# Band attention: weights of a 64-key half kept as 80 queries, sums and values as 64-row products in two slots around the next scores

## The chip, the cores and the metric

The kernel runs on one core of one Trainium2 chip. The metric is device microseconds for one execution, taken as the median of three runs. The kernel before takes 2633.2 us (the three runs: 2632.67, 2633.2 and 2638.77).

Engine names are those of the profile: PE is TensorE (matrix products), PEld its weight loads, DVE is VectorE, ACT is ScalarE, POOL is GpSimd, and SP issues the DMAs. Results of matrix products land in PSUM, which has eight banks of 128 partitions by 512 float32.

## The reference

The input is (2, 256, 128, 128) float32: batch, time, frequency, channel. Three blocks follow each other, each with a layer norm in front and a residual add behind it: attention over time (causal), attention over frequency (a band of 16 to each side), and a feed-forward net with gelu. Both attentions have four heads of 32 channels.

```python
xt = _ln(x, ln_t_w, ln_t_b).transpose(0, 2, 1, 3)
x = x + _mha(xt, t_wi, t_bi, t_wo, t_bo, H_T, cm).transpose(0, 2, 1, 3)   # causal
xf = _ln(x, ln_f_w, ln_f_b)
x = x + _mha(xf, f_wi, f_bi, f_wo, f_bo, H_F, bm)      # abs(i - j) <= 16
xn = _ln(x, ln_n_w, ln_n_b)
h = jax.nn.gelu(xn @ w1.T + b1, approximate=False)
x = x + (h @ w2.T + b2)
```

The change touches the second block alone, the band attention. There a sequence is 128 frequencies long, and a query sees only keys that are at most 16 away.

## The kernel before

Work goes in groups of 512 tokens (four sequences of 128). First come 128 groups of the time attention (class `OverTime`), then 16 runs, each of eight groups of the band attention (`OverBands`) and then eight of the feed-forward net (`FeedForward`). The loop in `run` walks over the groups; one turn n of it issues parts of several neighbouring groups, and `InOrder` pins every instruction to the place in its engine's queue where the program wrote it. So the order of calls in `run` is the order on each engine.

A float32 product on PE is written as one `matmul` and is recorded as two passes (two loads and two matmuls in the profile). The kernel always splits the array into smaller tiles which work side by side, one product in each. Three shapes matter here, written as rows (contracted) by columns (outputs):
- 128x32, four tiles, one for each head or each 32 output channels: projections, sums, values, output
- 32x64, eight tiles, four heads by two halves of the keys: scores
- 64x32, eight tiles, two halves of the keys by four heads: only in the change

What one band group does, in steps that the text below calls by these names:
- **projections** (`queries_keys`, `values`): qT and kT from two sets of four products of 512 columns, then v from 16 products of 128 columns. ACT takes them from PSUM.
- **scores** (`scores`): 32 products of 80 columns. A half of 64 keys meets only the 80 queries of its sequence that can be in its band; the bank holds 128 query columns for each sequence, and what lies outside the 80 is not written and masked later.
- **weights**: DVE puts the band of minus 1e30 on the last head (`scalar_tensor_tensor`, 128x512), ACT takes the exponential of all four heads (128x512 each), POOL then clears what is outside the band in the other three heads (`affine_select`, two each). The result is `pf`.
- **sums and values** (`weigh`): four products of 512 columns of `pf` with ones, then 16 of 128 columns of `pf` with v, over all 128 keys of a sequence.
- **division**: ACT takes ln and exp of the sums (`invert`, gives r), DVE refines and multiplies in three instructions (`divide`, gives oT).
- **output** (`output`, `finish`): 16 products of 128 columns, and the residual add on DVE.

In a turn n in the midst of a run the order on PE is: scores of group n, sums and values of n-1, output of n-2, queries and keys of n+1, values' projection of n+1. Where the first feed-forward group follows the last band group (`turn` in `run`), the sums and values of n-1 stand behind the hidden products of the feed-forward group.

PSUM banks are handed out in rotation (`turn_of_bank`), with some numbers reserved ahead (`held`, `follow`). A bank's next user waits until the last reader of the bank is done.

## Time and profile before

| | |
|---|---|
| median of three runs | 2633.2 us |
| span of the profiled execution | 2631.9 us |
| band groups, feed-forward groups, time groups | 128 each |
| sums of `pf`, passes of 128x512 | 1024, mean 603 ns |
| values of `pf`, passes of 128x128 | 4096, mean 273 ns |
| scores of the band groups, passes of 32x80 | 8192, mean 240 ns |
| `affine_select` on `pf`, POOL | 768, mean 637 ns |
| exponential to `pf`, ACT | 512, mean 602 ns |

The page of the profiled execution gives its span, from the first to the last instruction; the run's time has about 1.3 us beside it. A "mean" of a pass on PE is the time from its start to its end in the pipeline; since tiles work side by side and passes follow each other before they end, what a step costs is read from the starts of one step and the next in the timeline, and not from means times counts.

### The profile page before, as it was taken

The numbers are of one execution on the slowest core, as the hardware profiler recorded it, in microseconds if no ns is written. First come the engines' busy times: TensorE is split into PE (matmuls) and PEld (weight loads), VectorE is DVE, ScalarE is ACT, GpSimd is POOL, SyncE is SP. The second block draws the span as 40 slices with busy tenths as digits, with TensorE's granted clock in tenths as the row PEclk, the third lists the DMA queues.
The fourth block names the chain that finished last, engine by engine and source line by source line (L and its number), as shares of the span: only waits on it lengthen the run. The fifth ranks groups of instructions, "written<-read, shape, count | busy, mean of one in ns | idle before, by whom it ended". The sixth has DMA issues, their size and how long they took to land.

```text
span 2631.9 us, 156460 instructions
## 1 busy us (share of the span) xinstructions
PE 2617.8 (99%) x68688; PEld 1837.4 (70%) x68688; DVE 2140.8 (81%) x6410; ACT 1838.8 (70%) x3543; POOL 1958.6 (74%) x2311
## 2 busy tenths in 40 slices
PE   9999999999999999999999999999999999999999
PEld 6666666666766767666777776667676677777776
DVE  8888888888888887977878779788797797887974
ACT  7989988999899875564655746647557466475573
POOL 7999999999999987666667666665776666757762
PEclk9999999999999999999999999999999999999999
DMA  6656555565565454445454544554454445554543
GB/s 155 167 149 158 149 149 149 155 155 149 149 158 149 122 127 119 115 123 127 118 124 124 123 122 117 126 128 120 122 126 120 120 119 131 123 120 123 123 104 88
DMA packets 469797, 344.97 MB, mean 131 GB/s; under 512 B 43120, under 2 KB 404464, under 8 KB 469104
## 3 DMA queue, kind: packets, MB, share of 16 engines
q1 hardware_dynamic: 468408, 334.41, 50.5%
q8 instruction: 540, 8.85, 1.5%
q14 instruction: 153, 1.25, 0.2%
q10 hardware_dynamic: 696, 0.46, 0.1%
HBM read 167.98 MB, written 166.72 MB: 127 GB/s over the span
## 4 chain that ended last, share of the span: by engine, by line
PE 99%; DVE 0%; issue 0%; DMA 0%; ACT 0%; ACTq 0%; DVEq 0%
PE bank L907 99%; DMA x<-in_x 0%; DVE xh L907 0%; DVE bank L907 0%; DVE res L907 0%; DVE stats L907 0%; DVE oT L907 0%; DVE u L907 0%; DVE xnT L907 0%; ACTq L907 0%; ACT p L907 0%; DVE vy L907 0%; ACT lnv L907 0%; DVE mv L907 0%; ACT root L907 0%
## 5 line engine op out<-in xcount | busy, mean ns | idle before, releaser
L907 ACT ACTIVATE hT<-bank,b 128x512 f32<-128x512 f32 x512 | 348.1, 688 | 524.2 <-PE bank L907 483.2
L907 POOL TENSOR_SCALAR_AFFINE_SELECT pf<-pf 128x512 f32<-128x512 f32 x768 | 477.7, 637 | 185.3 <-ACT pf L907 159.1
L907 PEld LDWEIGHTS bank<-w2T_sb,hT 128*32 128x32 f32 x16384 | 467.4, 110 | 54.8 <-issue 29.0
L907 PE MATMUL bank<-xnT,wf 128*32 128x512 f32 x4096 | 492.4, 592 | 0.5 <-DVE xnT L907 0.5
L907 PE MATMUL bank<-xnT,w1f 128*32 128x512 f32 x4096 | 486.3, 592 | 0.2 <-issue 0.2
L907 PE MATMUL bank<-w2T_sb,hT 128*32 128x128 f32 x16384 | 482.8, 273 | 1.0 <-issue 1.0
L907 ACT ACTIVATE p<-bank 128x512 f32<-128x512 f32 (+1 forms) x1024 | 430.6, 494 | 62.9 <-PE bank L907 62.9
L907 DVE TENSOR_SCALAR xh<-x,mv,rstd 128x160 f32<-128x160 f32 (+1 forms) x1012 | 394.3, 432 | 59.7 <-POOL rstd L907 49.4
L907 POOL TENSOR_SCALAR_AFFINE_SELECT p<-p 128x1024 f32<-128x1024 f32 (+2 forms) x384 | 364.5, 949 | 57.5 <-ACT p L907 49.1
L907 PEld LDWEIGHTS bank<-wf,xnT 128*32 128x32 f32 x8192 | 243.3, 110 | 144.1 <-issue 101.6
L907 POOL TENSOR_TENSOR p<-p,p 128x512 f32<-128x512 f32 x256 | 324.6, 1291 | 10.6
L907 DVE BATCH_NORM_STATS2 stats<-x 128x6 f32<-128x128 f32 x1536 | 329.0, 276 | 3.4 <-DMA x<-in_x 3.4
L907 POOL TENSOR_SCALAR rstd<-mv 128x4 f32<-128x4 f32 x251 | 57.8, 230 | 361.7 <-DVE mv L907 360.5
L907 PEld LDWEIGHTS bank<-xnT,w1f 128*32 128x32 f32 x4096 | 183.6, 110 | 171.6 <-issue 109.6
L907 PE MATMUL bank<-qT,kT 32*64 32x80 f32 (+4 forms) x16384 | 302.0, 271 | 0.1
L907 PEld LDWEIGHTS bank<-qT,kT 32*64 32x64 f32 x16384 | 260.0, 131 | 51.2 <-ACT kT L907 50.6
L907 DVE TENSOR_TENSOR res<-bank,res 128x512 f32<-128x512 f32 (+1 forms) x259 | 170.3, 658 | 153.3 <-PE bank L907 144.7
L907 ACT ACTIVATE pf<-bank 128x512 f32<-128x512 f32 x512 | 265.8, 602 | 35.5 <-PE bank L907 31.3
L907 PE MATMUL bank<-wn,oT 128*32 128x128 f32 x8192 | 283.8, 274 | 0.1
L907 DVE STREAM_TRANSPOSE z<-xh 128x512 f32<-128x512 f32 x380 | 270.3, 711 | 13.3
L907 PE MATMUL bank<-wf,xnT 128*32 128x128 f32 x8192 | 276.5, 273 | 0.0
L907 POOL TENSOR_TENSOR rstd<-rstd,mhalf 128x4 f32<-128x4 f32 x251 | 260.8, 1039 | 20.9
(100 smaller groups left out, 3820.3 us busy)
## 6 DMA issues: line engine op xcount, KB each, us to landing
turned<-z SPq DMA_DIRECT2D x1520, 64.0 KB, 2.7
xnT<-turned SPq DMA_DIRECT2D x380, 256.0 KB, 3.2
x<-res SPq DMA_DIRECT2D x256, 128.0 KB, 2.5
x<-x SPq DMA_DIRECT2D x128, 256.0 KB, 4.1
out<-res SPq DMA_DIRECT2D x252, 128.0 KB, 2.3
x<-in_x SPq DMA_DIRECT2D x124, 256.0 KB, 4.3
x<-in_x SPq DMA_DIRECT2D x4, 128.0 KB, 2.8
x<-in_x SPq DMA_DIRECT2D x6, 64.0 KB, 2.9
```

Source lines behind the costliest of these rows:

```text
L907: return self.tc.keep_in_program_order(emit(*args, **kwargs))
```

## The change

The weights of a half of 64 keys are kept as 80 query columns (`REACH`), and so the scores' bank, the exponential and the masks handle 4 x 80 = 320 columns for each head. POOL multiplies with a constant `keep` of ones and zeros, once for a head in place of two selections. The head that DVE masks is now masked and exponentiated later in the turn (`late_mask`, `late_function`).

Sums and values are taken over 64 keys at a time, on 64x32 tiles, 80 queries each, and the two halves are added in PSUM where they overlap. The first slot (`weigh_first`) has the sums of the upper half and the values of the lower, the second slot (`weigh`) the sums of the lower and the values of the upper. The first slot of group n-1 stands ahead of the scores of n, the second behind them. At the end of a run the output of n-2 stands between the two slots. A copy of one column on ACT (`seen`) is issued behind the first slot, and the first product of the second slot waits for it.

Banks are no longer handed out in rotation but from a list of free ones, oldest first; each user gives its bank back when its last reader has been issued.

```diff
+REACH = HALF + BAND
-    by_vector = 1
+    by_vector = 3
-        self.sp = {h: path.bank([P, NT * P], "sp") for h in heads}
+        self.sp = {h: self.take(f"sp{h}", [P, NT, REACH]) for h in range(H)}
...
-                        self.sp[h][keys, q], self.kT[r, i * P + e * HALF : i * P + (e + 1) * HALF], self.qT[r, q],
-                        start=True, stop=True,
+                        self.sp[h][keys, i], self.kT[r, i * P + e * HALF : i * P + (e + 1) * HALF],
+                        self.qT[r, a : a + REACH], start=True, stop=True,
...
+    def first_mask(self):
+        path = self.path
+        keep = path.keep.unsqueeze(1).to_broadcast([P, NT, REACH])
+        for h in range(H):
+            if h != self.by_vector:
+                path.gpsimd.tensor_tensor(self.p[:, h], self.p[:, h], keep, ALU.mult)
...
+    def part(self):
+        path = self.path
+        seen = path.small.tile([P, 1], F32, name="seen")
+        self.seen = path.scalar.copy(seen, self.op_[:, NT - 1, 0:1])
...
+    def sums(self, e):
+        rows, a = slice(e * HALF, (e + 1) * HALF), e * (P - REACH)
+        for h in range(H):
+            m = self.path.tensor.matmul(
+                self.rp_[rows_of(h), :, a : a + REACH], self.path.k.ones[rows, 0:D], self.p[rows, h],
+                start=e == 1, stop=True, skip_group_check=True,
             )
+            if e == 0 and h == 0:
+                self.behind(m)
+
+    def weighted(self, e):
+        rows, a = slice(e * HALF, (e + 1) * HALF), e * (P - REACH)
         for i in range(NT):
             for h in range(H):
                 r = rows_of(h)
+                self.path.tensor.matmul(
+                    self.op_[r, i, a : a + REACH], self.v[rows, i, r], self.p[rows, h, i],
+                    start=e == 0 and i == 0, stop=True, skip_group_check=True,
+                )
+
+    def weigh_first(self):
+        self.rp_ = self.take("rp", [P, NT, P])
+        self.op_ = self.take("op", [P, NT, P])
+        self.rp, self.op = (t.rearrange("p i q -> p (i q)") for t in (self.rp_, self.op_))
+        self.sums(1)
+        self.weighted(0)
+        self.part()
+
+    def weigh(self):
+        self.sums(0)
+        self.weighted(1)
...
+            if bands[1] and bands[2]:
+                do(n - 1, "weigh_first")
             do(n, "first_half", "first_function", "first_mask")
...
+            do_at(n, OverBands, "late_mask")
+            if turn:
+                do(n - 1, "weigh_first")
+                do(n - 2, "output", "finish")
             do(n - 1, "weigh")
             do(n - 1, "invert_exactly" if turn else "invert")
+            do_at(n, OverBands, "late_function")
...
-            if bands[2] or turn:
+            if bands[2]:
                 do(n - 2, "output", "finish")
```

How this moves instructions is seen in three places, all in turns of the loop in the midst of a run. First PE, from the last two score products of a turn to the first ones of the next, before (`pf,ones` are the sums, `pf,v` the values, `wn` the output, `xnT,wf` queries and keys, `wf,xnT` the projection of v):

```order
L907 MATMUL bank_111<-qT,kT 64x80
L907 MATMUL bank_112<-qT,kT 64x80
L907 MATMUL bank_115<-pf,ones 32x512 x4
L907 MATMUL bank_108<-pf,v 32x128 x16
L907 MATMUL bank_113<-wn_241,oT 32x128 x16
L907 MATMUL bank_114<-xnT,wf_238 32x512 x4
L907 MATMUL bank_109<-xnT,wf_238 32x512 x4
L907 MATMUL bank_110<-wf_238,xnT 32x128 x16
L907 MATMUL bank_111<-qT,kT 64x80
L907 MATMUL bank_112<-qT,kT 64x80
```

and in the change:

```order
L968 MATMUL bank_114<-qT,kT 64x80
L968 MATMUL bank_115<-qT,kT 64x80
L968 MATMUL bank_109<-pf,ones 32x4x80 x4
L968 MATMUL bank_110<-pf,v 32x80 x16
L968 MATMUL bank_112<-wn_253,oT 32x128 x16
L968 MATMUL bank_113<-xnT,wf_250 32x512 x4
L968 MATMUL bank_111<-xnT,wf_250 32x512 x4
L968 MATMUL bank_108<-wf_250,xnT 32x128 x16
L968 MATMUL bank_114<-pf,ones 32x4x80 x4
L968 MATMUL bank_115<-pf,v 32x80 x16
L968 MATMUL bank_112<-qT,kT 64x80
L968 MATMUL bank_109<-qT,kT 64x80
```

The second slot of one group stands where sums and values stood, with 80 columns for 128; the first slot of the next group has come in ahead of the next scores. The scores now take banks 109 and 110, in which the sums and values of the group before were added up (their division reads them); before, they took other banks.

Second DVE, from one finished oT to the next, before (`band` is the mask, `xh` the normalization of a later group, `z` its transpose, `x` the residual add):

```order
L907 TENSOR_TENSOR oT<-bank_112,u 128x4x4x32
L907 SCALAR_TENSOR_TENSOR bank_110<-bank_110,band 128x512
L907 TENSOR_SCALAR xh<-x,mvs,rstds 128x5x32 x4
L907 STREAM_TRANSPOSE z<-xh 128x512
L907 TENSOR_TENSOR x_18417<-bank_111,x_18417 128x512
L907 TENSOR_TENSOR bank_113<-bank_113,r_20994 128x512
L907 SCALAR_TENSOR_TENSOR u<-bank_113,r_20994 128x512
L907 TENSOR_TENSOR oT<-bank_114,u 128x4x4x32
```

and in the change:

```order
L968 TENSOR_TENSOR oT<-bank_110,u 128x4x4x32
L968 TENSOR_SCALAR xh<-x,mvs,rstds 128x5x32 x4
L968 STREAM_TRANSPOSE z<-xh 128x512
L968 SCALAR_TENSOR_TENSOR bank_113<-bank_113,band 128x320
L968 TENSOR_TENSOR x_18429<-bank_111,x_18429 128x512
L968 TENSOR_TENSOR bank_114<-bank_114,r_21059 128x512
L968 SCALAR_TENSOR_TENSOR u<-bank_114,r_21059 128x512
L968 TENSOR_TENSOR oT<-bank_115,u 128x4x4x32
```

The mask has moved behind the normalization and its transpose, and has 320 columns.

Third ACT over one turn, before (`pf` are the exponentials):

```order
L907 COPY v<-bank_114 128x512
L907 ACTIVATE pf<-bank_115 128x512
L907 ACTIVATE pf<-bank_108 128x512
L907 ACTIVATE pf<-bank_109 128x512
L907 ACTIVATE pf<-bank_110 128x512
L907 ACTIVATE ln<-bank_113 128x512
L907 ACTIVATE r_20994<-ln 128x512
L907 ACTIVATE qT<-bank_112,bq_283 128x512
L907 COPY kT<-bank_115 128x512
```

and in the change:

```order
L968 COPY v<-bank_108 128x512
L968 COPY seen<-bank_115 128x1
L968 ACTIVATE pf<-bank_112 128x320
L968 ACTIVATE pf<-bank_109 128x320
L968 ACTIVATE pf<-bank_110 128x320
L968 ACTIVATE ln<-bank_114 128x512
L968 ACTIVATE r_21059<-ln 128x512
L968 ACTIVATE pf<-bank_113 128x320
L968 ACTIVATE qT<-bank_108,bq_295 128x512
L968 COPY kT<-bank_112 128x512
```

The copy `seen` stands ahead of the exponentials, and the last head's exponential has gone behind ln and r.

## The prediction, made before the change was run

> **What bounds the kernel now.** I read the page first: its busy shares and its chain.

> ```profile
> span 2631.9 us, 156460 instructions
> PE 2617.8 (99%) x68688; PEld 1837.4 (70%) x68688; DVE 2140.8 (81%) x6410; ACT 1838.8 (70%) x3543; POOL 1958.6 (74%) x2311
> PE 99%; DVE 0%; issue 0%; DMA 0%; ACT 0%; ACTq 0%; DVEq 0%
> ```

> PE is never idle and is the whole chain, so the change is worth what it does to PE, as long as no other engine takes over. Next the timeline of PE over one turn of the band stage, since the starts there give what each step costs:

> ```profile
> 1497.43 0.97 PE L907 MATMUL bank<-qT,kT 32*64 32x80 f32 x64
> 1498.33 1.06 PE L907 MATMUL bank<-pf,ones 128*32 128x512 f32 x8
> 1499.21 1.06 PE L907 MATMUL bank<-pf,v 128*32 128x128 f32 x32
> 1500.08 1.06 PE L907 MATMUL bank<-wn,oT 128*32 128x128 f32 x32
> 1500.95 1.90 PE L907 MATMUL bank<-xnT,wf 128*32 128x512 f32 x16
> 1502.67 1.06 PE L907 MATMUL bank<-wf,xnT 128*32 128x128 f32 x32
> 1503.66 0.97 PE L907 MATMUL bank<-qT,kT 32*64 32x80 f32 x64
> ```

> From start to start (us): scores 0.90, sums 0.88, values 0.87, output 0.87, queries and keys 1.72, projection of v 0.99; a turn is 6.23. Three things are to be seen. *The price of a column*: on each of four tiles the output makes 8 passes of 128 columns in 0.87 (109 ns a pass), queries and keys 4 of 512 in 1.72 (430 ns), so a pass costs a tile 0.84 ns a column and 2 ns: 69 ns for 80 columns, 0.27 us for 320. *A change of tile shape*: the projection of v has the same 32 passes as the output but costs 0.99, because another shape follows: 0.12 us. *A stall*: on eight tiles the 64 passes of the scores need 8 x 69 ns = 0.55 and cost 0.90.

> **The stall**, which decides this case. Narrow windows of the same timeline, up to 1503.99 and at 1503.99 and 1504.30 (rows begin with the first pass still under way):

> ```profile
> 1503.66 0.56 PE L907 MATMUL bank<-qT,kT 32*64 32x80 f32 x33
> 1503.78 0.85 PE L907 MATMUL bank<-qT,kT 32*64 32x80 f32 x56
> 1504.04 0.58 PE L907 MATMUL bank<-qT,kT 32*64 32x80 f32 x30
> L907 PE MATMUL bank<-qT,kT 32*64 32x80 f32 x8192 | 124.0, 240 | 0.1
> ```

> 33 passes, that is 17 products with their two, start in the first third of a microsecond. The next starts at 1504.04, 0.38 after the first. The first product's second pass starts at 1503.78 and takes about 0.23 (mean 240 ns), so it ends near 1504.01, 0.03 ahead. I read this as a queue with room for 17 products, filled while PE changes shape, in which a place is handed on 0.03 us after a product has ended; then the other 15 products enter at about 20 ns each.

> Are places handed on in program order, or as products end? In the band scores all products are alike and both give 0.90. In the time stage's scores they have 64 to 256 columns, and there it differs. I worked through their 32 products in the written order (`TIME_ORDER`), with the prices above: from the first score to the next step 1.30 us in program order, 1.18 in any order; the whole time turn 7.06 and 6.94.

> ```profile
> 501.67 1.39 PE L907 MATMUL bank<-qT,kT 32*64 32x64 f32 x64
> 502.98 1.08 PE L907 MATMUL bank<-wn,oT 128*32 128x128 f32 x32
> 508.75 1.14 PE L907 MATMUL bank<-qT,kT 32*64 32x64 f32 x41
> ```

> The rows have 1.31 and 7.08: program order. [...]

> **The change, PE.** A slot has four sums of 320 columns on one half of the rows and 16 values of 80 columns on the other. On eight tiles side by side a slot would need 2 x 0.27 or 8 x 69 ns: 0.55 us, where sums and values now have 1.75 together. But the sums stand first in program order and end late. Bounds of a 320-column pass from start to end:

> ```profile
> L907 PE MATMUL bank<-xnT,wf 128*32 128x512 f32 x4096 | 492.4, 592 | 0.5 <-DVE xnT L907 0.5
> L907 PE MATMUL bank<-p,ones 128*32 128x256 f32 x2048 | 134.0, 379 | 0.0
> L907 PE MATMUL bank<-pf,ones 128*32 128x512 f32 x1024 | 143.6, 603 | 0.0
> ```

> Between 379 ns at 256 columns and 592 at 512: 0.43 us at 320. The first sum's second pass starts at 0.29 (0.27 and some 0.025 for weights that could not be loaded ahead; 64-row tiles are not in this trace, and I take the 128-row ones, which have 32 columns too). It ends at 0.73, and its place goes on at 0.76. The queue holds four sums and 13 values. So the last three values enter at 0.76, 0.78 and 0.80, load for 0.03 and make two passes: the last pass starts at 0.90. By the rows of the scores the next shape starts 0.16 after the last pass. **A slot costs about 1.05 us**, 0.5 of it with most tiles empty.

> In a turn: scores 0.90 as before, 2 x 1.05 for 0.88 and 0.87, the rest unchanged (the 0.12 behind the projection of v stays; the change of shape behind each slot is in its 0.16). That is +0.35; worked through product by product it is 6.60 for 6.23, +0.37. There are seven such turns in each of 16 runs: 112 x 0.37 = **+41 us**. At a run's end the slots stand around the output, between steps of another shape: +0.35 and two changes at 0.12, 16 x 0.59 = **+9 us**. The bounds of a slot are 0.71 (0.55 + 0.16, no stall) and 1.27 (sums and values one after the other); I take 1.05, because the rule behind it gives 0.90, 1.31, 6.23 and 7.08 as the rows have them.

> **The other engines.** DVE now makes some turns longer than PE does:

> ```profile
> 1478.43 0.96 PE L907 MATMUL bank<-qT,kT 32*64 32x80 f32 x64
> 1484.97 0.97 PE L907 MATMUL bank<-qT,kT 32*64 32x80 f32 x64
> 1492.69 0.67 DVE L907 SCALAR_TENSOR_TENSOR bank<-bank,band 128x512 f32<-128x512 f32 x1
> 1497.57 0.69 DVE L907 TENSOR_TENSOR oT<-bank,u 128x512 f32<-128x512 f32 x1
> 1499.23 0.67 DVE L907 SCALAR_TENSOR_TENSOR bank<-bank,band 128x512 f32<-128x512 f32 x1
> ```

> Masks at 1492.69 and 1499.23 are 6.54 apart with DVE busy throughout, and one turn of PE is 6.54 (1478.43 to 1484.97). Such turns add some 0.6 us a run over 6.23, about 9 us in 16 runs (read alike in all runs; this row is one of them). With a mask of 320 columns for 512 DVE needs about 6.3. At 6.60 from PE it is no longer late: **-9 us**, at most; at least 0.

> New on the path could be the banks: scores of n+1 take the banks of the sums and values of n-1, and so wait for oT of n-1. That ends, after the scores of n start: scores 0.90, second slot with output 1.92, some 0.2, residual add 0.6 and three instructions at 0.7 each: 5.8. Against 6.60 that is free; it would decide in a shorter turn.

> ```profile
> L907 POOL TENSOR_SCALAR_AFFINE_SELECT pf<-pf 128x512 f32<-128x512 f32 x768 | 477.7, 637 | 185.3 <-ACT pf L907 159.1
> L907 POOL TENSOR_TENSOR p<-p,p 128x512 f32<-128x512 f32 x256 | 324.6, 1291 | 10.6
> L907 ACT ACTIVATE pf<-bank 128x512 f32<-128x512 f32 x512 | 265.8, 602 | 35.5 <-PE bank L907 31.3
> L907 ACT ACTIVATE p<-bank 128x256 f32<-128x256 f32 x512 | 183.6, 390 | 62.3 <-PE bank L907 62.3
> ```

> POOL's masks go from 6 x 0.64 = 3.8 to 3 x 0.81 = 2.4 (1291 ns by 320/512; between 0 and 3 x 1.29), ACT's four exponentials from 2.4 to 1.8 (0.44 each, between 390 and 602 ns). Both lie beside PE, and the first slot needs them only 5.6 after the scores start, so neither counts. The copy `seen` is bounded by 0 and a pass of 256 (390 ns); behind it on ACT stand the exponentials, which need the scores anyway, 0.9 later. Its waiter, the second slot, stands behind the scores: nothing. The late exponential stands behind ln and r and is done some 4 us after the scores start: nothing.

> Sum: 2631.9 + 41 + 9 - 9 = 2673 for the profiled span; with the 1.3 us by which the median lies above it, **2674**.

> **Rivals.**
> 1. *Places come free in any order, or 64-row tiles have more room.* Then a slot is 0.71, a PE turn 5.94, and DVE (6.3 with statistics) and the chain to oT (5.8 and a wait) set it to about 6.1, against 6.31 on average now (6.23 and 9 us over 112 turns). -0.2 x 112: 2610. For it: the eight tiles of the scores do run side by side. Against it: the 1.31 and 7.08. [...] Chance 0.15.
> 2. *The same, with the gain eaten* by DVE or by the wait for the banks: turns near 6.3, 2633 within 8. Chance 0.05.
> 3. *The wait for the banks decides too.* The row of the scores at 1491.20, to set beside that of oT at 1497.57 above:

> ```profile
> 1491.20 0.97 PE L907 MATMUL bank<-qT,kT 32*64 32x80 f32 x64
> ```

> There oT of n-1 ends at 1498.26, 7.1 after the scores of n start, with DVE late. In the change a normalization of 1.6 us and a transpose stand ahead of the mask; if DVE is late by them, this wait decides once oT ends more than 6.6 after its turn's scores start. Turns at 6.85 would give 112 x 0.25 more, 2702. Against it: DVE needs only 6.3. Chance 0.10.
> 4. *The row halves do not run side by side*, so that the change doesn't do what it says: a slot of 1.27, 128 x 2 x 0.22 more: 2730. For it: no row here has a 64-row tile. Against it: eight tiles of 32 rows do. Chance 0.04.

> **How the numbers follow.** The forecast, 2660 to 2690, has 0.66: places for 16 or 18 products move it by 4, the 9 us of DVE by 9. Rivals 1 and 2 have 0.20, rivals 3 and 4 0.14. The range from 2620 to 2705 takes in the forecast and rivals 2 and 3 (0.81), and leaves out rivals 1 and 4. Faster by over 0.3% (8 us, about what a measurement of this kernel can tell from no change): 0.15; within: 0.05; slower: 0.80.

> **What would show it.** In the changed kernel's timeline a slot should take 1.05 from its start to the next step, with 16 or 17 products started early, a gap until about 0.76, and then the last values; the next scores should keep 0.90, the turn should have 6.60. If slots have 0.7, the queue is not what I think; if slots have 1.05 and turns are longer than 6.7, look for loads of the scores that wait for DVE. I would be wrong most of all if 64-row tiles are handled otherwise than the two shapes that this trace has.

## The result, and the profile after

The changed kernel takes **2756.1 us** (median of four runs, 2749.0 to 2768.5) against 2633.4: a ratio of 1.047, with a 95% interval from 1.0446 to 1.0492. The forecast of a slower kernel was right, its size was not: 123 us where 41 were forecast, and outside the range. The profiled execution has a span of 2747.2 us, 115.3 above the one before.

The page of the changed kernel, its span, busy times, chain and the row of the DMA queue that brings instructions; the last row is that of the kernel before, for which the prediction did not quote it:

```profile
span 2747.2 us, 166900 instructions
PE 2688.8 (98%) x73808; PEld 1823.1 (66%) x73808; DVE 2124.2 (77%) x6410; ACT 1777.4 (65%) x3671; POOL 1804.0 (66%) x1934
q8 instruction: 581, 9.52, 1.6%
PE 95%; issue 2%; DVE 2%; DMA 0%; ACT 0%; SPq 0%; POOL 0%; ACTq 0%; DVEq 0%; POOLq 0%
```

```profile
q8 instruction: 540, 8.85, 1.5%
```

PE still is the chain, but it is no longer never idle: "issue", time in which it waits for nothing that the profile shows, has 2%. Two numbers will matter: PE has 5120 matmuls more, and as many loads, together 10240 records; and q8 has 41 packets more.

The timeline of PE over one undisturbed turn, to set beside the turn that the prediction shows:

```profile
1741.48 0.97 PE L968 MATMUL bank<-qT,kT 32*64 32x80 f32 x64
1742.38 0.47 PE L968 MATMUL bank<-pf,ones 64*32 64x320 f32 x4
1742.41 0.48 PE L968 MATMUL bank<-pf,v 64*32 64x80 f32 x16
1742.67 0.45 PE L968 MATMUL bank<-pf,ones 64*32 64x320 f32 x4
1742.71 0.78 PE L968 MATMUL bank<-pf,v 64*32 64x80 f32 x16
1743.42 1.08 PE L968 MATMUL bank<-wn,oT 128*32 128x128 f32 x32
1744.32 1.90 PE L968 MATMUL bank<-xnT,wf 128*32 128x512 f32 x16
1746.04 1.06 PE L968 MATMUL bank<-wf,xnT 128*32 128x128 f32 x32
1747.02 0.47 PE L968 MATMUL bank<-pf,ones 64*32 64x320 f32 x4
```

The scores keep 0.90, a slot takes 1.04 (1742.38 to 1743.42), and the next turn begins at 1748.07: 6.59. That is the forecast turn. The gap is there too, best seen on the weight loads of the same slot (PEld):

```profile
1742.43 0.54 PEld L968 LDWEIGHTS bank<-pf,v 64*32 64x32 f32 x22
1743.13 0.17 PEld L968 LDWEIGHTS bank<-pf,v 64*32 64x32 f32 x6 [0.17 <-issue]
```

The last six loads, those of three values, start 0.75 after the start of the slot, where 0.76 was forecast.

Most turns are not like this one: of the 80 turns 3 to 7 only 23 take 6.6 or less. The turn just ahead of it took 9.24 us:

```profile
1732.24 0.97 PE L968 MATMUL bank<-qT,kT 32*64 32x80 f32 x64
...
1734.18 1.07 PE L968 MATMUL bank<-wn,oT 128*32 128x128 f32 x28
1737.51 0.30 PE L968 MATMUL bank<-wn,oT 128*32 128x128 f32 x2 [2.27 <-issue]
1737.52 0.62 PE L968 MATMUL bank<-xnT,wf 128*32 128x512 f32 x2
1737.64 0.28 PE L968 MATMUL bank<-wn,oT 128*32 128x128 f32 x2
...
1741.48 0.33 PE L968 MATMUL bank<-qT,kT 32*64 32x80 f32 x8
```

In the midst of the output, 28 of its 32 passes made, PE stops for 2.27 us. The other four passes need nothing that the 28 did not need: the same oT, the same bank. Who was waited for, in the view of waits, after and then before (us in total, times, longest):

```profile
PEld bank L968 <- issue: 616.6, 2032, 2.6
PE bank L968 <- issue: 42.5, 54, 2.3
PE bank L968 <- DVE ok L968: 1.7, 1, 1.7
```

```profile
PEld bank L907 <- issue: 450.6, 1567, 1.7
PE bank L907 <- issue: 4.4, 9, 1.3
```

No engine and no DMA that the program issued stands behind these stops. The view counts full idleness only; against an undisturbed turn, turns 3 to 7 alone lose 0.72 x 80 = 57 us (table below).

After a few stops there is a second price. The stretches around a stop of 2.3 us that ends at 1421.21 (busy times of PE, PEld, DVE, ACT and POOL with their instructions, then the granted clock of PE, the share of DMA and GB/s):

```profile
1418.70:1421.20 2.50, 0.22 (x7) 0.00 (x0) 0.45 (x2) 0.98 (x3) 1.73 (x3) 1.00 0.40 78
1421.20:1422.00 0.80, 0.79 (x18) 0.68 (x22) 0.04 (x1) 0.00 (x0) 0.00 (x0) 1.00 0.66 137
1422.00:1425.40 3.40, 3.40 (x32) 1.96 (x28) 3.33 (x8) 1.06 (x2) 0.00 (x0) 0.50 0.39 129
1425.40:1430.00 4.60, 4.58 (x203) 3.74 (x197) 3.04 (x11) 2.82 (x8) 2.65 (x4) 1.00 0.16 40
```

For 3.4 us PE has half its clock, which I estimate at 1.7 us of lost time. The clock's record in the trace has 0.50 for 3.4 us after three of the stops (those of 1.42, 2.29 and 2.22 us that end at 950.23, 1421.21 and 2547.68), each time from 0.8 us after the stop's end, 5 us of lost time together by that estimate, and once after a wait of 1.70 us for DVE that ends at 1024.96; in the kernel before it has none until PE's last product is done. After the stop of 2.27 us that ends at 1737.51 the clock stayed at 1.00. What sets the clock back was not tried.

The 115 us by place, from the distances between the first score passes of one group and the next in the two timelines, means over 16 runs:

| | before | after | more, over 16 runs |
|---|---|---|---|
| first turn of a run | 7.25 | 8.35 | 18 us |
| turns 2 to 7, each | 6.17 | 7.06 | 85 us |
| run end (last scores to the next run's first) | 61.90 | 62.70 | 13 us |

And the same from turns without a stop: first turn 7.12 and 8.16, a turn 6.23 and 6.58, run end 61.71 and 61.56. That is 1.04 + 6 x 0.35 - 0.15 = 3.0 a run, **48 us**: the term that the prediction had as 41 + 9. The other **67 us** are stops and, for 5 to 7 of them, half clock, beyond what the kernel before has of them; the prediction had -9 there.

### The profile page after: what moved, and what is told of

Same layout as the page of the kernel before. It is cut to its first block, busy times and chain, and to the rows that moved or that the text cites. A ratio compares the mean times of both kernels' runs of the same rounds, so it can differ in the third digit from the quotient of the medians.

```text
span 2747.2 us, 166900 instructions
## 1 busy us (share of the span) xinstructions
PE 2688.8 (98%) x73808; PEld 1823.1 (66%) x73808; DVE 2124.2 (77%) x6410; ACT 1777.4 (65%) x3671; POOL 1804.0 (66%) x1934
## 4 chain that ended last, share of the span: by engine, by line
PE 95%; issue 2%; DVE 2%; DMA 0%; ACT 0%; SPq 0%; POOL 0%; ACTq 0%; DVEq 0%; POOLq 0%
PE bank L968 95%; DVE xh L968 0%; DVE stats L968 0%; DVE res L968 0%; DMA out<-res 0%; DMA x<-x 0%; DVE ln L968 0%; DMA x<-in_x 0%; DVE mv L968 0%; DVE z L968 0%; DMA turned<-z 0%; DVE gs L968 0%; DVE x L968 0%; DVE tests L968 0%; SPq L968 0%
## 5 line engine op out<-in xcount | busy, mean ns | idle before, releaser
L968 POOL TENSOR_TENSOR pf<-pf,keep 128x320 f32<-128x320 f32 x384 | 323.4, 873 | 337.7 <-ACT pf L968 337.6
L968 PE MATMUL bank<-xnT,wf 128*32 128x512 f32 x4096 | 501.0, 597 | 5.4 <-issue 2.9
L968 PEld LDWEIGHTS bank<-w2T_sb,hT 128*32 128x32 f32 x16384 | 452.7, 110 | 71.9 <-issue 46.7
L968 PE MATMUL bank<-xnT,w1f 128*32 128x512 f32 x4096 | 472.2, 593 | 2.8 <-DVE ok L968 1.7
L968 PE MATMUL bank<-w2T_sb,hT 128*32 128x128 f32 x16384 | 473.7, 273 | 1.3 <-issue 1.3
L968 PE MATMUL bank<-pf,v 64*32 64x80 f32 x8192 | 267.5, 234 | 13.7 <-issue 11.7
L968 PEld LDWEIGHTS bank<-xnT,w1f 128*32 128x32 f32 x4096 | 132.5, 110 | 212.8 <-issue 183.8
```

What stands on the lines that cost most here:

```text
L968: return self.tc.keep_in_program_order(emit(*args, **kwargs))
```

## The experiments

Theory Q is the prediction's: PE's queue with 17 places in program order. The theory that the stops called for is F (it was formed on the profile after): a product costs PE not only time but four records (two loads, two matmuls; a record is one instruction of PE as the profile lists it), and PE's instructions are brought in pieces by queue q8, no faster than some rate. The page gives a piece: 10240 records more with 41 packets more, and in the kernels below 8192 more with 32, 10240 fewer with 40: 256 records in 16 KB. The rival that the prediction had kept for a longer turn is the wait for banks.

### e1: the sums in the midst of a slot

The four sums of a slot are put between its values, so that by Q no long product stands at the queue's head when it is full.

```diff
-        self.sums(1)
-        self.weighted(0)
+        self.weighted(0, (0, 1))
+        self.sums(1)
+        self.weighted(0, (2, 3))
```

(and likewise in the second slot, whose wait on `seen` moves to its first value product)

> The change, but in each slot the first eight value products are written ahead of the four sums and the other eight behind them. Queue in program order (theory): the products that hold places longest are no longer the oldest, so the stall inside a slot goes: a slot takes 0.70 us in place of 1.04, an undisturbed turn 5.9 in place of 6.58. Rival (64-row tiles are slow by themselves, or sums and values hinder each other): the slot stays at about 1.04 and the turn at 6.58. Total: without the stalls that come from outside 2747 - 16 x 16 x 0.34 = 2660; if these stalls are PE's instruction supply, they grow, since the same instructions are used up faster: 2640 to 2690 in all.

Measured: 2746.8 us (ratio 1.0426, 1.0408 to 1.0443), far above the 2640 to 2690 that were expected. Timeline of PE:

```profile
1741.27 0.27 PE L970 MATMUL bank<-pf,v 64*32 64x80 f32 x4
1741.32 0.47 PE L970 MATMUL bank<-pf,ones 64*32 64x320 f32 x4
...
1742.00 1.08 PE L970 MATMUL bank<-wn,oT 128*32 128x128 f32 x32
...
1744.61 0.40 PE L970 MATMUL bank<-wf,xnT 128*32 128x128 f32 x7
1746.39 0.92 PE L970 MATMUL bank<-wf,xnT 128*32 128x128 f32 x25 [1.38 <-issue]
```

The slot falls from 1.04 to 0.73 with the same products, where Q had 0.70 and the rival 1.04. An undisturbed turn is 5.95, and by it the kernel would beat the one before (6.23). But the last two rows have the other half: PE stops amid a projection, and the mean of turns 2 to 7 is 7.09, against 7.06 in the change. What Q gave back, the stops took:

```profile
PE bank L970 <- issue: 93.8, 89, 2.9
```

42.5 us in the change, 93.8 here, and eight stretches of half clock for four (mean granted clock 0.994 for 0.997).

### e2: the next scores take other banks

The banks of sums and values are given back only after the next scores have taken theirs, so the scores need not wait for oT of the group before.

```diff
-        self.give("rp", "op")
+        self.give_late("rp", "op")      # back on the free list after the next scores' take
```

> The change, with the banks of sums and values handed back only after the next scores have taken theirs, so that scores never wait for the division of the group before. Theory (the 75 us over the undisturbed turns are PE waiting for its instructions): no change, 2740 to 2765, turns still up to 8 to 10 us. Rival (scores wait for the banks): the excess goes, 2675 to 2690, nearly all turns 6.58.

Measured: 2758.6 us (one run), mean of turns 2 to 7 7.16, longest 11.52: no gain, where the rival (2675 to 2690) asked for some 70 us. The wait for banks plays no part; this rival falls.

### e3 and e4: the kernel before with more products

Products of one column are added to the band scores of the kernel before, 16 or 32 a group, on columns that are masked later. They add PE time at the scores, which is seen there, and records; no bank, no mask and no slot of the change is in them.

```diff
+                c = i * P + (1 - e) * (P - 1)
+                for h in heads[:TINY // 8]:
+                    path.tensor.matmul(self.sp[h][keys, c : c + 1], ..., self.qT[r, c : c + 1], start=True, stop=True)
```

> The kernel before with 16 more score products of one column in each band group (108 products a turn for 92; the change has 112), into places that are masked later. Their own work on eight tiles is small, but places in the queue and the stage's length grow: an undisturbed turn about 6.45 to 6.6. Theory (instruction supply): turns far above the undisturbed one appear, with a fetch of instructions 2 to 3 us ahead of each resumption; mean turn 0.2 to 0.5 over the undisturbed, total 2680 to 2720. Rival (stalls come from the slots, their banks or the copy): turns stay within 0.1 of the undisturbed one on average, 2660 to 2675.

> The same with 32 products of one column (124 a turn). Theory (instruction supply): more than twice the excess of 16, mean turn 0.4 to 0.8 over an undisturbed 6.8 to 6.95, total 2740 to 2790. Rival: turns within 0.1 of the undisturbed one, 2690 to 2710.

Measured: 2704.7 and 2816.3 us (one run each); the second is above the 2740 to 2790 that were expected. An undisturbed turn of e4 in the timeline:

```profile
1306.12 1.69 PE L915 MATMUL bank<-qT,kT 32*64 32x80 f32 x128
1307.74 1.06 PE L915 MATMUL bank<-pf,ones 128*32 128x512 f32 x8
...
1313.07 0.35 PE L915 MATMUL bank<-qT,kT 32*64 32x80 f32 x10
```

The scores now take 1.62, so a turn should take 6.95 (6.23 + 0.72). Turns 3 to 7 have a mean of 7.68, and only 4 of those 80 are undisturbed. In the waits of e4:

```profile
PE bank L915 <- issue: 54.6, 82, 1.9
```

against 4.4 in the same kernel without the added products. So the stops can be made without anything of the change but more records. e3 has a part of it: 6.59 undisturbed, 6.90 in the mean.

### e5: the change with fewer products

Projections and output of the band stage go on two tiles of 128x64 in place of four of 128x32: half the products, the same columns. A turn has 92 products, as many as the kernel before.

```diff
+    if wide:
+        for c in range(2):
+            r = slice(c * HALF, (c + 1) * HALF)
+            path.tensor.matmul(out[r], weights[:, r], x, start=start, stop=stop)
+        return
```

> The change, with the band groups' projections and output on two tiles of 128x64 in place of four of 128x32: half the products (20 for 40 a turn, 92 in all for 112), the same columns in all. Theory (PE uses up its instructions faster than they are fetched, some 62 to 64 records a microsecond at most): 368 records a turn need 5.8 us, under the 6.58 of the work, so the long turns go, mean turn 6.6 to 6.7, total 2680 to 2695. Rival (the excess comes from something else in the slots): total stays 2740 to 2760. If a pass on a 128x64 tile costs more a column, the projections are longer in the timeline (output 0.9, queries and keys 1.7, v 0.9 now), and this is read off there.

Measured: 2718.3 us (one run). An undisturbed turn is 6.59, as in the change, and 54 of 80 turns now are undisturbed; the mean of turns 3 to 7 falls from 7.30 to 6.95. The waits:

```profile
PE bank L972 <- issue: 18.3, 18, 2.8
```

The direction is that of F. The size is not: the time lies between what F (2680 to 2695) and the rival (2740 to 2760) asked for, and the kernel before, with as many products in a shorter turn, loses a quarter of that (0.09 a turn, here 0.36). So the number of records a turn is not all.

### e6 and e8: sums in the middle and fewer products

Both edits together (e6), and with e2's as well (e8).

> Sums in the middle of a slot, and the projections and output on 128x64 tiles (92 products a turn). Theory: the slot takes 0.72, the undisturbed turn 5.9, and 368 records a turn are fetched in 5.8, so both gains show: turns of 5.9 to 6.3 (DVE needs 6.3 where it has statistics), total 2595 to 2630, faster than both kernels. Rival (fetching is no bound): as with 112 products, 2745.

> The sixth kernel with the banks of sums and values handed back after the next scores have theirs. With turns of 5.9 the wait of the scores for the division of the group before (about 5.8 after its turn's scores) may now be felt: 0 to 15 us faster than the sixth, 2590 to 2625; equal to it if DVE or the fetch sets the turn.

Measured: 2659.0 us (1.0091, 1.0073 to 1.0108) and 2659.0 (1.0095, 1.0078 to 1.0112). Both miss the expectation (2595 to 2630 and 2590 to 2625). Undisturbed 5.96 in both, mean of turns 3 to 7 6.48 and 6.46: here too the banks don't matter. Taking 20 products a turn out of e1 is worth 88 us. Still the kernel isn't faster than before, and the stops alone account for it. Added up from undisturbed turns (first, second, five more and the run end), a run of e6 has 7.99 + 5.09 + 5 x 5.96 + 61.22 = 104.1 us, against 7.12 + 5.36 + 5 x 6.23 + 61.71 = 105.3 before, so without stops it would gain some 20 us in 16 runs.

### e7: the kernel before with fewer products

The same edit on the kernel before alone: 72 products a turn.

> Control: the kernel before with the same 128x64 projections and output (72 products a turn for 92). Theory: PE's work is the same, and what waits there were for instructions (9 us over 6.23 a turn) go: 2618 to 2633. If a pass costs more on 128x64 tiles, it is slower by 40 columns' worth of steps: over 2700.

Measured: 2656.0 us (1.0084, 1.0067 to 1.0101). It is slower, where 2618 to 2633 were expected, since a change of tile shape now stands between values and output: values and output cost 0.12 and 0.05 more a turn, and an undisturbed turn is 0.15 longer, 17 us in 112 turns. A run end is 0.8 longer (62.68), 13 us. The stops that went, 0.09 in each of 80 turns, gave back 7 us. Its timeline:

```profile
1692.31 0.97 PE L911 MATMUL bank<-qT,kT 32*64 32x80 f32 x64
1693.21 1.06 PE L911 MATMUL bank<-pf,ones 128*32 128x512 f32 x8
1694.09 1.06 PE L911 MATMUL bank<-pf,v 128*32 128x128 f32 x32
1695.08 1.09 PE L911 MATMUL bank<-wn,oT 128*64 128x128 f32 x16
1696.00 1.89 PE L911 MATMUL bank<-xnT,wf 128*64 128x512 f32 x8
1697.72 1.04 PE L911 MATMUL bank<-wf,xnT 128*64 128x128 f32 x16
1698.69 0.32 PE L911 MATMUL bank<-qT,kT 32*64 32x80 f32 x8
```

6.38, and 79 of 80 turns have just that. Its waits have no row of PE for issue at all, and on the weight loads the longest is 0.4 us (1.7 before, 2.6 in the change):

```profile
PEld bank L911 <- issue: 602.5, 2104, 0.4
```

This is the cleanest of the runs: fewer records, no stops. And it shows something of the kernel before. Its masks still have 512 columns and DVE works as much as before (2140.9 us busy, 2140.8 before), yet 79 of 80 turns are 6.38.

So the long turns that the prediction laid to DVE were not DVE's. The trace of the kernel before says the same. The prediction set two stretches of 6.54 side by side, but they are not the same turn. While DVE is busy throughout, from the mask at 1492.69 to the one at 1499.23, PE makes its turns in 6.23 (scores at 1491.20, 1497.43 and 1503.66, rows that the prediction shows). In PE's turn of 6.54, from 1478.43 to 1484.97, DVE waits for PE, and PE pauses among the loads for queries and keys without a wait:

```profile
1479.58 0.70 DVE L907 SCALAR_TENSOR_TENSOR bank<-bank,band 128x512 f32<-128x512 f32 x1 [0.64 <-PE bank L907]
```

```profile
1481.85 0.23 PEld L907 LDWEIGHTS bank<-xnT,wf 128*32 128x32 f32 x4
1482.26 0.25 PEld L907 LDWEIGHTS bank<-xnT,wf 128*32 128x32 f32 x6 [0.18 <-issue]
```

A packet of q8 had started at 1479.79, 2.47 ahead of the resumption. Of all 21 turns 3 to 7 of that kernel that are over 0.05 longer than 6.23, none waits for DVE. Thirteen have such pauses within a step; in seven, each the last turn of its run, the sums wait for a mask of POOL, by 0.16 at most; in one the next projection waits for ACT, by 0.1.

### e9 and e10: the same products, spread

In e1 and e6 the next group's query projection (few, long products) is moved between the first slot and the scores, so that the many short products don't come in one burst. By mean rate nothing should change, by bursts much.

```diff
+            ahead = bands[1] and bands[2] and bands[3]
+            if ahead:
+                do(n + 1, "queries", "take_query")
             do(n, "first_half", "first_function", "first_mask")
```

> Sums in the middle of a slot as in the first experiment, all products on the tiles of the change (112 a turn), but the queries' projection of the next group (four products of 512 columns, 0.86 us) moved to stand between the first slot and the scores. PE's work gains one change of shape: an undisturbed turn 6.05 to 6.1. Same number of records a turn, spread more evenly. If a turn is bound by the mean rate of the fetches (62 to 64 records a microsecond): still about 7.0 a turn and 2735 to 2750. If it is bound by bursts that use up 256 records (slot, scores, slot: about 2.3 us) faster than a fetch takes: most of the excess goes, mean turn 6.2 to 6.6, 2645 to 2700.

> The same order with 92 products a turn (projections and output on 128x64 tiles). Undisturbed turn 6.15. Either way little excess is left: by the mean rate 368 records need 5.8, by bursts there are none: mean turn 6.2 to 6.35, total 2640 to 2665, about equal to the sixth experiment; under 2633 only if DVE's turns with statistics no longer count.

Measured: 2728.9 us (1.0361, 1.0329 to 1.0392) and 2664.2 (1.011, 1.0091 to 1.0129). Turns 3 to 6 hold the same products as before the move. Their mean falls from 7.45 to 7.09 and from 6.46 to 6.38, although an undisturbed turn is 0.14 to 0.15 longer; what is lost over the undisturbed turn falls from 1.50 to 1.00 and from 0.50 to 0.27. So bursts count; but in e9 stops remain:

```profile
PE bank L975 <- issue: 49.3, 82, 2.0
PE bank L975 <- POOL pf L975: 3.1, 11, 0.3
PE bank L975 <- DVE oT L975: 2.3, 11, 0.3
```

By the expectations of e9, its mean turn is what a mean rate gives (448 records / 7.09 = 63 a microsecond), and its total lies between the two cases. The total of e10 is in its range (2640 to 2665), its mean turn just above (6.2 to 6.35). The total gains little or nothing (e10 is 5 us above e6, e9 18 below e1), since a turn pays for one change of shape more, and stops remain. The first turn of each run is 0.9 to 1.0 longer (9.01 for 8.13, 9.15 for 8.11), but that is no loss: it holds one query projection more, and the seventh turn one less. Here, in turns near 6.1, the waits for oT and pf appear that the prediction had placed at 5.8 and 5.6: eleven times each in e9, and small.

### What the ten kernels say together

Turns 3 to 7 of the 16 runs (3 to 6 in e9 and e10, whose seventh has no query projection). "Alone" is the shortest turn (in e9 only two of 64 turns come within 0.03 of it), "wanted" are four records a product by that, "mean" is the mean turn and "stops" the difference:

| | products | alone, us | wanted, per us | mean, us | stops, us |
|---|---|---|---|---|---|
| e7 | 72 | 6.38 | 45 | 6.39 | 0.01 |
| e5 | 92 | 6.59 | 56 | 6.95 | 0.36 |
| before | 92 | 6.23 | 59 | 6.32 | 0.09 |
| e10 | 92 | 6.11 | 60 | 6.38 | 0.27 |
| e6 | 92 | 5.96 | 62 | 6.48 | 0.52 |
| e3 | 108 | 6.59 | 66 | 6.90 | 0.31 |
| change | 112 | 6.58 | 68 | 7.30 | 0.72 |
| e4 | 124 | 6.95 | 71 | 7.68 | 0.73 |
| e9 | 112 | 6.09 | 74 | 7.09 | 1.00 |
| e1 | 112 | 5.95 | 75 | 7.37 | 1.42 |

At 45 records a microsecond there are no stops; from about 60 on they grow, by and large, with what is wanted, and where 66 or more are wanted, what is had stays between 61 and 65 (448 / 7.30 = 61 in the change, 448 / 7.37 = 61 in e1, 496 / 7.68 = 65 in e4). The order is not strict: the kernels with slots lose more than those without at a like number (e5 and e6 against the kernel before and e3). The starts of q8's packets in the trace say the same from the other side. In the band runs of the change and of e1 one in a hundred of their distances is under 3.35 us, half are under 3.9 to 4.0, and the mean is 4.1: 256 / 4.1 = 62 records a microsecond. In e7 the mean is 5.6: nothing presses.

Around the stop shown above, the packets' starts and the time they took (us):

```
1728.99 0.96
1734.70 1.39
1738.68 0.99
1742.65 0.88
1746.12 1.29
```

The packet at 1734.70 comes 5.71 after the one ahead of it, and PE, which had stopped by 1735.3, goes on at 1737.51, 2.81 after that packet started. The undisturbed turn from 1741.48 has packets 3.5 to 4.0 apart. In turns 2 to 7 of the change 121 gaps between starts on PE are over 0.12 us longer than the same gap is in the median of the 16 runs (66 us in all). Of these, 77 with 54 us end 2.2 to 3.2 us after a packet's start, where chance would put about a quarter of them (1.0 of 4.1 us); the three longest (2.48, 2.48 and 2.45) end 2.98, 2.71 and 2.81 after one.

e5 stands furthest out of the order. What sets it apart from the kernel before is where its records lie: slot, scores and slot are 72 products or 288 records in 2.98 us (97 a microsecond, more than a whole packet), where scores, sums and values of the kernel before are 208 in 2.65 (78). That this density is the reason was not tried in e5 itself; e9 and e10 speak for it.

## Why the prediction was wrong

- **PE bounds the kernel; price of a column, change of shape:** right. A pass of 320 columns took 441 ns (0.43 taken), the projection of v ahead of another shape 0.98 (0.99), the output in the turn above 0.90 (0.87). The 0.025 and 0.03 us for a load were estimates; the weight loads of the kernel before have 26.3 us for 1024 of the sums (0.026 each) and 467.4 for 16384 of `w2T_sb,hT` (0.029). 64-row tiles run side by side as assumed (a slot of 1.04, where one after the other would be 1.27).
- **The queue with 17 places in program order:** its times were right, and it is the heart of the reasoning. Slot 1.04 (1.05), undisturbed turn 6.58 (6.60), and e1, which only reorders, gives 0.73. Three values of 16 came late in the slot, as 17 places have it; 16 or 18, which the forecast allowed for, would have left four or two. No row shows the queue itself: it is a reading of these times. Rivals 1 and 2 fall with the slot: 0.7 needs another order of products, and there the stops take the gain.
- **+41 and +9:** 48 us measured for 50, though placed otherwise: the first turn of a run has +1.04 and not +0.37, the run end -0.15 and not +0.59. A run's first slot stands in its first turn, so that three slots (3.1 us) are left for the run end, where sums and values stood twice (3.5). The sum over a run does not depend on the place: each of the eight groups has two slots in place of one step of sums and values.
- **-9 us, "DVE now makes some turns longer than PE does":** this is the step that failed. The prediction took a stretch of DVE and a turn of PE for the same because both have 6.54, but DVE's stretch lies beside PE turns of 6.23, and in PE's turn of 6.54 DVE waited for PE (e7, above). The long turns were stops of PE. So there was nothing to win from a shorter mask, and the cause of the 9 us was one that the change makes worse. The view of waits of the kernel before had 4.4 us of "issue" on PE, and the prediction did not ask what they were.
- **The sum as a whole:** it weighed each added product by its PE time. It had no term for 20 products more a turn as instructions: 448 records where 368 were, with 59 a microsecond already wanted. "PE is never idle" was taken to mean that only its work counts. Measured as the 67 us that are not the queue's, in place of -9. With this term at +67, the sum is 2631.9 + 48 + 67 = 2747, the profiled span; that is the measured split added up again, not a test of it.
- **Rivals 3 and 4** had longer times, 2702 and 2730, by mechanisms that are ruled out: the banks by e2 and e8, the row halves by the slot. Their times lay nearer to the measured one than the forecast, for other reasons.
- **POOL, ACT, `seen`:** hidden, as said. Masks took 873 ns (810), exponentials 435 (440), `seen` 159 (under 390).

That the stops are a matter of PE's records is shown by e3 and e4 (with records added to the kernel before, they come) and by e7 (with records taken out, they go). That q8's packets bring these records is shown by the packet counts; that a late packet ends the stop is read from the trace, not tried. Open is what limits the packets: a rate, or the time from a start to the first usable record against bursts. e9 was to tell them apart and came out between. Open too is why a packet starts late, as at 1734.70; whether the program's own DMA traffic delays packets was not tried.

No version here beats the kernel before. The nearest are e7 and e6, 0.8 and 0.9% slower.

## What to carry to other kernels

Count PE's records as well as its columns: where a change trades few long products for many short ones, divide the records of a turn by its time, and set that beside what the kernel has now (here 59 a microsecond was nearly free, 68 cost a tenth of the turn). A small "issue" row for PE in the view of waits, of 4.4 us, was the sign here that this limit was close: from 59 to 68 records a microsecond it grew tenfold, to 42.5. With the same products less in one burst (e9 for e1, e10 for e6) a turn lost 1.00 for 1.50 and 0.27 for 0.50. And before a long turn of PE is laid to an engine that is busy, see that both are in the same stretch of time, and which of the two waited.
